# Two-layer graph attention: where three pieces of work at the crossing from layer 0 to layer 1 are issued

## The chip, the cores and the metric

The kernel runs on one core of one Trainium2 chip. The metric is the device time of one execution in microseconds, the median of several runs. A core has five engines that work side by side: TensorE (PE, matrix products into PSUM), VectorE (DVE), ScalarE (ACT), GpSimd (POOL) and SyncE (SP), whose queue here issues most transfers. Each engine executes its own instructions in the order in which the program emits them, and waits on semaphores for the others.

## What is computed

Eight batches of 2048 nodes with 256 features pass through two graph layers that share one adjacency matrix. Each is wrapped as `x = x + layer(relu(layernorm(x)))`. Layer 0 is attention with four heads, normalised separately in each chunk of 256 keys; layer 1 is attention of the additive kind, whose logit is a leaky ReLU of one number per query and one per key.

```python
h = jnp.maximum(_layernorm(x, axis=-1), 0.0)
# layer 0: q, k, v = h @ W.T; scores clipped to +-10, absent edges at -10
attn = jax.nn.softmax(scores, axis=-1)            # within each chunk of 256 keys
out = ctx @ Wo.T + bo + h
x = x + layernorm(out) * gamma + beta
# layer 1
h = jnp.maximum(_layernorm(x, axis=-1), 0.0)
hW = h @ W
e = leaky_relu(e_src[:, :, None] + e_dst[:, None, :], 0.01)
e = jnp.where(adj == 0, -1e9, e)
x = x + relu(softmax(e) @ hW)
```

A node without any edge gets equal weights in layer 1, so its output is the plain mean of `hW` over all nodes. The kernel treats these nodes apart: it adds up `h` over the nodes of a batch, multiplies the sum by `W` once, and adds the result where a node is alone.

## The kernel before

**Tiling.** Everything is done in fp32 on 128 partitions. The 2048 nodes of a batch are four blocks of 512 (called `zero`, `low`, `mid`, `last` in the main loop), a block is four tiles of 128 tokens. PSUM has eight banks in use: four in two double tiles with the tag `s` (`ps_s`; `ps_h` takes the first half of one), two with the tag `n`, two with the tag `t`. The function `ps_m` hands out `t`, or, while `turn_about` is set, `n` and `t` in turn.

**Layer 0.** `Attention.begin` (L597) and `Attention.end` (L629) emit one step of attention together: 32 steps, each 512 queries against a chunk of 256 keys. A step's products are the logits (L490), the values (L506) and the sums of exponentials (L518), all on quarter tiles of the array, so that several run at once. VectorE clips (L530), ScalarE takes exponentials (L539), GpSimd adds halves (L545), `invert` takes the reciprocal on ScalarE (L550, L551), and `scale` (L560) on VectorE multiplies values by it, which frees the `n` banks. `gather` (L565) then adds the product to the context by a transfer issued from GpSimd. `fence` (L462) puts a wait by way of SP between two groups of matmuls that write the same bank.

The steps are software-pipelined: at the end `begin(33)`, `end(33)` and `begin(34)` have no new logits and only finish values and sums of the last two steps.

**Pieces beside attention.** A dictionary `todo` holds pieces of other work by half step: `at(STEPS2 + 2, ...)` is emitted in `begin(33)`, `STEPS2 + 3` in `end(33)`, `STEPS2 + 4` in `begin(34)` and run in `end(34)`, `STEPS2 + 5` in `end(34)`. A piece marked `pe` is emitted between the exponentials and the scaling in `begin`, and in `end` ahead of the fenced second half of the sums. If there is a next batch (`ahead`), its first projections are put there as `pe` pieces, in banks from `ps_h`.

**Between the layers.** Class `Between` carries a block from its context to layer 1. `output` and `take` multiply by `Wo` and add the residual; `stats`, `power`, `shift`, `scaled`, `gamma`, `beta`, `add` are the layer norm and the addition; `stats1`, `power1`, `shift1`, `norm1` the next norm. Its result is turned to have features on partitions: either on TensorE (`turn1`, L375, and `keep1`, L786, which also adds up the features), or by `flip1`, `send1`, `fetch1`, a path through DRAM, after which `sum1` (L803 to L809) adds up each half on ScalarE. `values(t)` (L811 to L817) is the product of one token tile with the layer-1 weights, in 258 columns: the features and both attention numbers. `keep(t)` (L819) copies the features to `g` on ScalarE (L822) and the two numbers to `sd` on VectorE (L823). `ends(1)` is `values` and `keep` for all four tiles. `sum1` writes its copy over its own input, except for a block whose `flip1` was given the tag "both".

**Layer 1.** `Layer1.weights` (L936) builds four key tiles of weights at a time on VectorE in a tile of five buffers, from the source of the block (`source`, L919, on ScalarE) and the targets. `products` (L956, L963) multiplies them with `g`. There are 16 such pieces per batch, four per block; `weights(i + 2)` is emitted before `products` of piece `i`. `total` (L896) reduces the sums of features on VectorE, `mean` (L885) multiplies them by the weights on TensorE (L890) and copies the result on ScalarE (L894), and `alone` (L968) adds it on VectorE, at the third piece of each block. `early(i)` is `products` of piece `i` issued ahead of the main loop.

**Order.** The order at the crossing is written out by hand, in two branches: `if ahead` (batches one to seven) and `else` (the eighth). After the last product of a crossing, layer 1 runs in a loop over the 16 pieces, with the first steps of the next batch's attention at its end. All four compute engines and SP follow this order (`manual_schedule`).

Of the kernel before, what the change touches and what calls it, by code (L numbers as in the profile page):

```python
# [28 lines left out]
def gnn_two_layers(  # L29
# [26 lines left out]
    TB = NB // P  # L56
# [14 lines left out]
    def ps_n():  # L71
        return ps.tile([P, 512], F32, tag="n", name="ps_n")

    def ps_t():
        return ps.tile([P, 512], F32, tag="t", name="ps_t")
# [4 lines left out]
    def ps_m():  # L80
        if turn_about[0]:
            turn_about[1] += 1
            if turn_about[1] % 2:
                return ps_n()
        return ps_t()
# [128 lines left out]
    def pe(piece):  # L214

        piece.kind = "pe"
        return piece
# [161 lines left out]
    class Projection:  # L379
# [40 lines left out]
        def fetch(self, nb):  # L420
            self.hT[nb] = Features(turned_d[0][nb])
# [18 lines left out]
        def values(self, nb):  # L440
            if self.v is None:
                self.v = work.tile([P, NT, F], F32, tag="v", name="v", bufs=1)
            for t2 in range(TB // 2):
                pp = ps_m()
                for i in range(2):
                    t = 2 * t2 + i
                    for di in range(FC):
                        nc.tensor.matmul(  # L448
                            pp[:, i * F:(i + 1) * F], self.hT[nb].tokens(di, t), wvT[:, di, :],
                            start=di == 0, stop=di == FC - 1,  # L450
                        )
                t0 = nb * TB + 2 * t2
                nc.vector.tensor_tensor(
                    self.v[:, t0:t0 + 2, :], pp.rearrange("p (i f) -> p i f", i=2),
                    bv_r[:, None, :].to_broadcast([P, 2, F]), op=ALU.add,
                )
# [216 lines left out]
    class Between:  # L673
# [134 lines left out]
                    spare = self.turning.squares.rearrange("p f t b -> p (f t b)")[:, c * NB:(c + 1) * NB]  # L808
                nc.scalar.activation(spare, h, AF.Copy, accum_out=self.sums[:, self.nb, c:c + 1])  # L809

        def values(self, t):  # L811
            pp = self.pp[t] = ps_m()
            for di in range(FC):
                nc.tensor.matmul(  # L814
                    pp[:, 0:F + 2], self.hT.tokens(di, t), w1s[:, di, :],
                    start=di == 0, stop=di == FC - 1,
                )  # L817
# [182 lines left out]
    STEPS2 = 2 * STEPS  # L1000
# [46 lines left out]
    for nb in range(NNB - 1):  # L1047
        i = 6 * nb
# [69 lines left out]
    for b in range(B):  # L1118
# [3 lines left out]
        zero, low, mid, last = blocks  # L1122
        ahead = projs.get(b + 1)
        one = Layer1(b, blocks, sd, sums)
# [4 lines left out]
        def at(n, *pieces):  # L1129
            todo.setdefault(n, []).extend(pieces)  # L1130
# [46 lines left out]
        if ahead:  # L1177
            at(STEPS2 - 4, lambda: ahead.fetch(0))
            at(STEPS2 + 2, pe(lambda: ahead.tiles()), pe(lambda: ahead.qk(0, 0, ps_h)))
            at(STEPS2 + 3, pe(lambda: ahead.qk(0, 1, ps_h)), lambda: ahead.fetch(1))  # L1180
        else:
            at(STEPS2 - 4, zero.fetch1)
            at(STEPS2 + 4, zero.sum1)
        at(STEPS2 + 5, low.sum1)
        turn_about[0] = False
        for n in sorted(todo):
            if n < 4:
# [15 lines left out]
        if ahead:  # L1203
            for t in range(TB):
                mid.stats1([t])
                low.values(t)
                low.keep(t)
            zero.fetch1()
            mid.power1()
            mid.shift1()  # L1210
            mid.norm1(0)
            mid.norm1(1)
            ahead.values(0)
            ahead.fetch(2)
            last.output(0)
            last.output(1)
            mid.flip1(0, "both")
            last.take(0)
            mid.flip1(1)
            last.take(1)  # L1220
            mid.send1()
            zero.sum1()
            last.stats(range(TB))
            ahead.qk(1, 0)
            last.power()
            last.shift()
            last.scaled(range(TB))
            ahead.qk(1, 1)
            for t2 in range(2):
                last.gamma(t2)  # L1230
                last.add(t2)
            for t in range(TB):
                last.stats1([t])
                zero.values(t)
                zero.keep(t)
            mid.fetch1()
            last.power1()
            last.shift1()
            last.norm1(0)
            last.norm1(1)  # L1240
            ahead.values(1)
            ahead.qk(2, 0)
            last.flip1(0, "both")
            last.flip1(1)
            last.send1()
            ahead.fetch(3)
            mid.sum1()
            ahead.qk(2, 1)
            mid.ends(1)
            last.fetch1()  # L1250
            one.send(1)
            one.send(2)
            ahead.values(2)
            one.receive(1)
            one.targets(0, 3 * TB)
            one.sources(0)
            ahead.qk(3, 0)
            weights(0)
            ahead.qk(3, 1)
            last.sum1()  # L1260
            last.ends(1)
            one.total()
            one.targets(3 * TB, NT)
            weights(1)
            one.mean()
            one.send(3)
            ahead.values(3)
        else:
            for t in range(TB):
                zero.values(t)  # L1270
                zero.keep(t)
                mid.stats1([t])
            one.targets(0, TB)
            one.sources(0)
            mid.power1()
            mid.shift1()
            low.ends(1)
            weights(0)
            mid.norm1(0)
            mid.norm1(1)  # L1280
            one.targets(TB, 2 * TB)
            last.output(0)
            last.output(1)
            weights(1)
            last.take(0)
            last.take(1)
            mid.ends(0)
            mid.ends(1)
            last.stats(range(TB))
            last.power()  # L1290
            last.shift()
            last.scaled(range(TB))
            one.targets(2 * TB, 3 * TB)
            one.send(1)
            one.receive(1)
            accs[0] = one.accumulators(0)
            early(0)
            for t2 in range(2):
                last.gamma(t2)
                last.add(t2)  # L1300
            last.stats1(range(TB))
            last.power1()
            last.shift1()
            weights(2)
            last.norm1(0)
            last.norm1(1)
            early(1)
            last.ends(0)
            last.ends(1)
            early(2)  # L1310
            one.total()
            one.targets(3 * TB, NT)
            weights(3)
            one.mean()
            one.received(1)
            one.send(2)
            one.send(3)
            one.receive(2)
            weights(4)
# [4 lines left out]
        for i, (nb, j4) in enumerate(pieces1):  # L1324
            if not ahead and i < 3:
                continue
            if i + 2 < len(pieces1):
                weights(i + 2)
            if nb not in accs:
                accs[nb] = one.accumulators(nb)  # L1330
            if j4 == 1 and nb + 1 < NNB:
                one.received(nb + 1)
                if nb + 2 < NNB:
                    one.receive(nb + 2)
            if j4 == 2:
                one.alone(nb)
            one.products(accs[nb], ws.pop(i), j4)
            if j4 == 0 and nb > 0:
                one.finish(nb - 1, accs[nb - 1])
            if j4 == 0 and nb > 0 and nb + 1 < NNB:  # L1340
                fetch(bounds1, nb + 1)
            if ahead and (nb, j4) == (NNB - 1, 0):
                fetch(bounds, 0)
            if j4 == 1 and nb > 0:
                one.store(nb - 1)
            if far and i in (3, 6, 9, 12):
                far.send(i // 3 - 1)
            if far and i in (0, 3, 6, 9):
                far.load(i // 3)
            if far and i in (1, 4, 7, 10):  # L1350
                far.stats(i // 3, range(TB))
                far.power(i // 3)
                far.shift(i // 3)
            if far and i in (2, 5, 8, 11):
                for t2 in range(2):
                    far.norm(i // 3, t2)
                for t2 in range(2):
                    far.flip(i // 3, t2)
            if ahead and i == len(pieces1) - 4:
                att = Attention(ahead)  # L1360
            if ahead and i >= len(pieces1) - 4 and i < len(pieces1) - 1:
                att.early(i - (len(pieces1) - 4))
                if i == len(pieces1) - 2:
                    att.early(3)
# [34 lines left out]
```

## Time and profile before

| | |
|---|---|
| median of 3 runs | 3558.47 us (3555.39 to 3564.36) |
| the profiled execution's own time | 3563.89 us |
| its span in the trace | 3562.1 us |
| mean granted TensorE clock | 0.998 |
| logits L490, busy | 1431.8 us, 16384 records of 590 ns |
| values L506, busy | 1224.9 us, 16384 records of 591 ns |
| layer-1 products L963 in the s banks | 447.8 us, 2048 records of 380 ns |
| layer-1 values L814 in the t banks | 69.3 us, 256 records |
| product of the mean L890 | 8.7 us, 32 records |

Times are microseconds from the start of the span unless marked otherwise. A line of a timeline gives the start, the length, engine, source line, operation, output and inputs, shapes, and how many records were merged; in brackets stands how long the engine sat idle before it, and what ended that. One fp32 product appears as two records, and records overlap, since matmuls are pipelined: what a group costs is read from the start of one group to the start of the next. In a list of waits, "5.8, 7, 0.8" is the total, the number of times and the longest.

### The profile page before, as it was taken

To read this page: it belongs to the slowest core of one execution; us is meant where nothing else is said; L and a number is where in the kernel's file an instruction comes from. 1 tells how busy PE (TensorE), PEld (TensorE's weight loads), DVE (VectorE), ACT (ScalarE), POOL (GpSimd) and SP (SyncE) were. 2 spreads that over 40 slices of the span, in tenths; PEclk is the share of its full clock that TensorE was granted. 3 is DMA by queue.
4 is the path that set the end of the run, shared out by engine and by line. 5 is a ranking of instruction groups with operands and counts; after the bars stand their busy time and mean duration, and the time that the engine had idled before them with its cause. 6 is when DMAs were issued, how large, how long until landed. Compare 5 with 4: busy or idle time off the path is not lost.

```text
span 3562.1 us, 104433 instructions
## 1 busy us (share of the span) xinstructions
PE 3527.6 (99%) x46080; PEld 2183.0 (61%) x46080; DVE 2639.0 (74%) x3979; ACT 1947.4 (55%) x2961; POOL 1808.9 (51%) x1182
## 2 busy tenths in 40 slices
PE   8999999999999999999999999999999999999999
PEld 5455785557755577555775557655586555855568
DVE  7888677867678676786767867678586785757866
ACT  6677426763267633676236762367624766147750
POOL 2688016870278702786037850378404784048731
PEclk9999999999999999999999999999999999999999
DMA  7545423444234441344423444234442434124321
GB/s 234 119 107 134 87 74 85 91 113 91 80 79 85 123 95 60 85 96 109 92 66 85 97 110 91 71 79 91 120 103 55 91 81 118 57 55 91 85 69 48
DMA packets 169111, 329.74 MB, mean 93 GB/s; under 512 B 35664, under 2 KB 97360, under 8 KB 160464
## 3 DMA queue, kind: packets, MB, share of 16 engines
q1 hardware_dynamic: 127696, 203.51, 19.2%
q0 software_dynamic: 32640, 118.50, 18.0%
q8 instruction: 360, 5.90, 0.7%
q10 hardware_dynamic: 8320, 1.05, 0.2%
q14 instruction: 95, 0.78, 0.1%
HBM read 154.14 MB, written 51.43 MB: 58 GB/s over the span
## 4 chain that ended last, share of the span: by engine, by line
PE 97%; DVE 1%; DMA 1%; ACT 1%; issue 0%; POOL 0%; ACTq 0%; DVEq 0%; POOLq 0%; SPq 0%
PE ps_s L490 25%; PE ps_n L506 24%; PE ps_s L963 12%; PE ps_t L518 7%; PE ps_n L963 6%; PE ps_t L963 6%; PE ps_t L714 2%; PE ps_t L434 2%; PE ps_n L434 2%; PE ps_s L434 2%; PE ps_t L814 2%; PE ps_n L814 2%; PE ps_t L448 1%; PE ps_n L448 1%; DVE z L277 0%
## 5 line engine op out<-in xcount | busy, mean ns | idle before, releaser
L530 DVE SCALAR_TENSOR_TENSOR e<-ps_s,bound 128x1024 f32<-128x1024 f32 x1024 | 1224.1, 1220 | 404.0 <-PE ps_s L490 400.6
L545 POOL TENSOR_TENSOR both<-e 128x1024 f32<-128x1024 f32 x512 | 1219.8, 2407 | 571.1 <-PE ps_t L518 355.6
L490 PE MATMUL ps_s<-q,k 64*32 64x512 f32 x16384 | 1431.8, 590 | 1.5 <-DVE e L530 1.4
L539 ACT ACTIVATE e<-e 128x1024 f32<-128x1024 f32 x1024 | 1050.6, 1050 | 481.1 <-DVE e L530 462.7
L506 PE MATMUL ps_n<-e,v 64*32 64x512 f32 x16384 | 1224.9, 591 | 2.4 <-DVE prod L560 2.4
L506 PEld LDWEIGHTS ps_n<-e,v 64*32 64x32 f32 x16384 | 460.9, 107 | 473.1 <-issue 384.1
L490 PEld LDWEIGHTS ps_s<-q,k 64*32 64x32 f32 x16384 | 459.5, 106 | 448.6 <-issue 331.2
L518 PE MATMUL ps_t<-both,ones 64*32 64x512 f32 x4096 | 537.9, 592 | 0.1
L963 PE MATMUL ps_s<-g,w 128*128 128x257 f32 x2048 | 447.8, 380 | 0.0
L963 PEld LDWEIGHTS ps_s<-g,w 128*128 128x128 f32 x2048 | 388.8, 190 | 56.3
L560 DVE TENSOR_TENSOR prod<-ps_n,rz 128x512 f32<-128x512 f32 x448 | 288.5, 686 | 162.8 <-PE ps_n L506 96.1
L986 POOL TENSOR_TENSOR x<-x,r 128x256 f32<-128x256 f32 x124 | 90.7, 745 | 466.2 <-ACT r L984 465.4
L946 DVE SCALAR_TENSOR_TENSOR w<-bound,w 128x1024 f32<-128x1024 int8 x256 | 314.7, 1229 | 8.7
L354 POOL TENSOR_TENSOR krn<-krn,mv 128x4 f32<-128x4 f32 x28 | 6.8, 242 | 575.4 <-DVE w L940 575.4
L963 PE MATMUL ps_n<-g,w 128*128 128x257 f32 x1024 | 292.4, 382 | 0.0
L963 PE MATMUL ps_t<-g,w 128*128 128x257 f32 x1024 | 289.7, 380 | 0.0
L550 ACT ACTIVATE rz<-ps_t 128x512 f32<-128x512 f32 x256 | 152.6, 596 | 229.4 <-PE ps_t L518 201.5
L940 DVE TENSOR_SCALAR w<-src,cd 128x512 f32<-128x512 f32 x512 | 263.1, 556 | 7.0 <-ACT src L921 6.6
L963 PEld LDWEIGHTS ps_n<-g,w 128*128 128x128 f32 x1024 | 192.8, 190 | 44.3 <-issue 17.6
L565 POOL DMA_DIRECT2D ctxT<-prod x224 | 191.0, 853 | 54.1 <-DVE prod L560 46.7
L963 PEld LDWEIGHTS ps_t<-g,w 128*128 128x128 f32 x1024 | 193.8, 189 | 28.2
L551 ACT ACTIVATE rz<-rz 128x512 f32<-128x512 f32 x256 | 161.4, 630 | 8.2
(133 smaller groups left out, 2910.4 us busy)
## 6 DMA issues: line engine op xcount, KB each, us to landing
ctxT<-prod POOLq DMA_DIRECT2D x224, 512.0 KB, 4.9
bound<-bound_d SPq DMA_DIRECT2D x62, 1024.0 KB, 6.2
turned_d<-squares SPq DMA_DIRECT2D x232, 128.0 KB, 2.4
hT<-turned_d SPq DMA_DIRECT2D x58, 512.0 KB, 4.3
rows<-in_adj_dram SPq DMA_DIRECT2D x32, 512.0 KB, 5.3
x<-in_x_dram SPq DMA_DIRECT2D x32, 512.0 KB, 4.9
out_dram<-x SPq DMA_DIRECT2D x31, 512.0 KB, 2.6
xp<-in_x_dram SPq DMA_DIRECT2D x28, 512.0 KB, 4.5
```

The lines of the kernel that those rows point to most:

```text
L434: nc.tensor.matmul(in_key_order(pp) if i == 0 else pp, w[:, di, do * P:(do + 1) * P], h, start=di == 0, stop=di == FC - 1,)
L490: nc.tensor.matmul(self.s[n, o][c * Q:(c + 1) * Q, kt, :], self.k[p][rows, at:at + Q], self.q[p][rows, nb * NB:(nb + 1) * NB], start=True, ...
L506: made.append(nc.tensor.matmul(self.num[n, c][h * Q:(h + 1) * Q, :], self.v[rows, j * KT + kt, at:at + Q], self.e[n, p][rows, i * KT + kt, :],
L518: nc.tensor.matmul(self.total[n][h * Q:(h + 1) * Q, :], ones[rows, :], self.both[n, h // 2][rows, h % 2, :], start=half == 1, stop=half == 0,)
L530: nc.vector.scalar_tensor_tensor(self.e[n, p][:, i * KT:(i + 1) * KT, :], self.s.pop((n, o)), -CLIP * SC, bounds[nb][:, j * KT:(j + 1) * K ...
L539: nc.scalar.activation(e, e, AF.Exp, scale=1.0 / SC)
L545: nc.gpsimd.tensor_tensor(self.both[n, p], e[:, 0], e[:, 1], op=ALU.add)
L560: nc.vector.tensor_tensor(dst[:, c, :], self.num.pop((n, c)), self.rz[n], op=ALU.mult)
L565: nc.gpsimd.dma_start(self.ctxT[nb], self.prod.pop(n), accum_op=ALU.add)
L940: nc.vector.tensor_scalar(w[:, i, :], self.src[nb], self.cd[:, 0, j:j + 1], self.cd[:, 1, j:j + 1], op0=ALU.mult, op1=ALU.max,)
L946: nc.vector.scalar_tensor_tensor(two, bounds1[nb][:, j - 1:j + 1, :], 0.0, two, op0=ALU.is_gt, op1=ALU.mult)
L963: nc.tensor.matmul(accs[t][:, 0:F + 1], w[:, i, t * P:(t + 1) * P], g[:, j, :], start=j == 0, stop=j == NT - 1,)
```

## The change

Three things are issued elsewhere; nothing that is computed changes.

1. In the last batch, the layer-1 values of the first block (`zero.values` and `zero.keep` for its four tiles) become `pe` pieces of the last two attention steps, two in `begin(33)` and two in `end(33)`, with banks from `ps_h`. They leave their place after attention. `mid.stats1`, which was interleaved with them, now follows `targets` and `sources`.
2. `low.sum1` is no longer emitted at half step `STEPS2 + 5` for any batch. With a next batch it follows low's values and their copies, ahead of `zero.fetch1`. In the last batch it follows `low.ends(1)`, ahead of the first `weights(0)`; there also the two `last.take` (the residual sums) go ahead of the second weights, `weights(1)`.
3. With a next batch, `one.mean()` is emitted in layer 1 after the products of the first piece, not before `one.send(3)` and the next batch's `values(3)`. In the last batch it stays where it was.

```diff
-        def values(self, t):
-            pp = self.pp[t] = ps_m()
+        def values(self, t, bank=ps_m):
+            pp = self.pp[t] = bank()
...
         else:
+            def zero_values(t):
+                zero.values(t, ps_h)
+                zero.keep(t)
+
             at(STEPS2 - 4, zero.fetch1)
+            at(STEPS2 + 2, pe(lambda: zero_values(0)), pe(lambda: zero_values(1)))
+            at(STEPS2 + 3, pe(lambda: zero_values(2)), pe(lambda: zero_values(3)))
             at(STEPS2 + 4, zero.sum1)
-        at(STEPS2 + 5, low.sum1)
...
                 low.values(t)
                 low.keep(t)
+            low.sum1()
             zero.fetch1()
...
             weights(1)
-            one.mean()
             one.send(3)
             ahead.values(3)
         else:
-            for t in range(TB):
-                zero.values(t)
-                zero.keep(t)
-                mid.stats1([t])
             one.targets(0, TB)
             one.sources(0)
+            mid.stats1(range(TB))
             mid.power1()
             mid.shift1()
             low.ends(1)
+            low.sum1()
             weights(0)
             mid.norm1(0)
             mid.norm1(1)
             one.targets(TB, 2 * TB)
             last.output(0)
             last.output(1)
-            weights(1)
             last.take(0)
             last.take(1)
+            weights(1)
...
             one.products(accs[nb], ws.pop(i), j4)
+            if ahead and i == 0:
+                one.mean()
```

## The prediction

> **What bounds the kernel now.** I read the page's table of busy time first, then the chain of waits, then every wait of TensorE, and then the timeline of TensorE at one crossing from attention to layer 1 (the seventh batch) and at the last batch's.
>
> ```profile
> PE 3527.6 (99%) x46080; PEld 2183.0 (61%) x46080; DVE 2639.0 (74%) x3979; ACT 1947.4 (55%) x2961; POOL 1808.9 (51%) x1182
> ...
> PE 97%; DVE 1%; DMA 1%; ACT 1%; issue 0%; POOL 0%; ACTq 0%; DVEq 0%; POOLq 0%; SPq 0%
> ```
>
> TensorE is busy nearly all the time and 97% of the chain. A moved matmul costs the same elsewhere, so only time in which TensorE stands still, or runs at a lower clock, can be won. The reader is to see how few waits there are:
>
> ```profile
> PE ps_n L890 <- DVE hsum L898: 5.8, 7, 0.8
> ...
> PE ps_n L814 <- DVE o L728: 3.1, 1, 3.1
> PE ps_t L814 <- ACT hT L809: 2.4, 7, 0.3
> PE ps_n L506 <- DVE prod L560: 2.4, 2, 1.4
> ```
>
> Two waits occur 7 times, once in each batch that has a next one: the mean's product waits for the reduced sums, and the second block's values (low, L814) wait for low's sum on ScalarE. The other two lie in the last batch. A crossing with a next batch:
>
> ```profile
> 2981.45 2.27 PE L506 MATMUL ps_n<-e,v 64*32 64x512 f32 x28
> 2984.07 1.31 PE L814 MATMUL ps_t<-w1s,hT 128*128 128x258 f32 x4 [0.35 <-ACT hT L809]
> 2985.22 1.03 PE L814 MATMUL ps_n<-w1s,hT 128*128 128x258 f32 x4
> ...
> 3032.28 1.03 PE L814 MATMUL ps_t<-w1s,hT 128*128 128x258 f32 x4
> 3034.14 1.10 PE L890 MATMUL ps_n<-w1s,hsum 128*128 128x256 f32 x4 [0.83 <-DVE hsum L898]
> 3035.08 1.89 PE L448 MATMUL ps_t<-wvT,hT 128*128 128x256 f32 x8
> ```
>
> The starts matter more than the bracketed waits. The last batch's tail, and the clock granted in it:
>
> ```profile
> 3405.40 2.20 PE L506 MATMUL ps_n<-e,v 64*32 64x512 f32 x28
> 3409.04 3.68 PE L506 MATMUL ps_n<-e,v 64*32 64x512 f32 x32 [1.44 <-DVE prod L560]
> ...
> 3437.00 1.57 PE L814 MATMUL ps_n<-w1s,hT 128*128 128x258 f32 x4 [3.14 <-DVE o L728]
> ```
> ```profile
> 3406.80:3410.20 3.40, 1.96 (x32) 1.00 0.98 296
> 3410.20:3413.60 3.40, 3.40 (x32) 0.51 1.00 286
> 3413.60:3417.00 3.40, 3.30 (x28) 0.50 0.33 61
> 3417.00:3420.40 3.40, 3.40 (x32) 0.99 0.03 5
> 3434.10:3437.50 3.40, 0.50 (x2) 1.00 0.00 0
> 3437.50:3440.90 3.40, 3.40 (x9) 0.51 0.13 53
> ```
>
> (Columns of the second: stretch, length, TensorE busy, clock, DMA share, GB/s.) After each gap TensorE ran at half clock for 3.4 or 6.8 us.
>
> **What the Trainium skill says.** (1) "TensorE: Matmul & The Clock Gate", Part 1: the array's clock is either half or full, set from activity in a free-running window of 3413 ns. The trace agrees in the two values and in the length: 0.50 for two windows from 3410.2 and one from 3437.5. It differs in that a window with 1.96 us of work in it already led to the lower clock. (2) "PSUM — Partial Sum Buffer", PSUM bank collisions: the compiler back end adds a dependency between ScalarE and VectorE accesses of one bank, reads included. The trace agrees: VectorE's copy of two columns (L823) starts at 3420.59, just after ScalarE's copy of that bank (3420.20 + 0.36). (3) "Perfetto Trace Analysis", Identifying the Most-Contended Engine: matmul busy time is a poor measure because matmuls are pipelined. So I count from starts.
>
> **The mean inside layer 1 (7 batches).** From the last block's fourth L814 unit (3032.28) to the next batch's values (3035.08) are 2.80 us. A unit of L814 (one token tile, four records) lasts 0.87 from start to start (2985.22 to 2986.09), so without the mean the values could start at 3033.15: 1.93 earlier. Between products the mean takes 0.87: the last batch has it there already (starts 3466.46 and 3467.33). Net 1.06 a batch; 2.80 also stands at 410.87 − 408.07 and 846.78 − 843.98. 7 × 1.06 = 7.4 us. Cover: ScalarE's copy of the mean now waits for products(0), near 3036.6 + 6.94 = 3043.5 plus 0.87, and behind it on ScalarE waits the source of the next block, 0.71 us, done near 3045.5. VectorE needs that source for the fifth weights at 3048.1, and `alone` needs the mean at 3052.5. VectorE is also more than 10 us ahead of TensorE there (fifth weights done 3052.5, wanted near 3065). PSUM: the values take the banks of L814 copies done by 3032.5. If all cover failed, the old 1.06 would come back.
>
> **Low's sum after low's values (7 batches).** The first L814 unit takes 2984.07 to 2985.22. Unblocked it starts when the last attention values leave room: L434 followed the same x28 group after 2970.95 − 2968.81 = 2.14, stretched by 0.07 here, so at 2983.66, and a full-array unit after tiled ones costs 0.87 + 0.20 (the eight L434 after that group take 3.63 from start to start in the chain of waits, where four within a row take 1.72, eight 3.43). It ends at 2984.73: 0.49 earlier, 3.4 us in seven. What may come late instead: output's context. Its gather is issued at 2985.43 and lands 4.8 later, at 2990.2; output starts at 2991.29, in the changed kernel 2990.8. Enough, though with 0.6 us left. On ScalarE the two sums (1.22) now stand between the copies and `power1`: copies end near 2987.9, sums at 2989.2, `power1` at 2989.2 instead of 2988.90. VectorE's shift, first values, flips and takes queue behind it, 0.3 late; the bank that needs `take` first is wanted at 2997.7 and free at 2993.9. On SP, the fetch for zero reuses low's buffer: issued near 2989.3 instead of 2988.08.
>
> **The last batch.** Zero's four L814 units (3.5 us) move ahead. Two go after the values at 3405.40, into the gap before 3409.04. But their copies are queued ahead of the `scale` products on VectorE, and ScalarE's copy comes first: units at 3407.2 and 3408.07 end 3408.2 and 3409.1, the second ScalarE copy 3409.5, VectorE's 3409.7, first product done 3410.4 (0.69). TensorE's next values wait for that bank: 3410.4 instead of 3409.04. So 1.74 of work goes in, and a gap of 1.5 stays. Warm, those values take 1.7 plus 0.5 for the second bank (3412.6), sums 0.4, then the other two units (1.74) stand where TensorE now waits 0.95 for the fence (3413.58 to 3414.53), and the last sums and values take 2.15: attention ends near 3416.8, not 3418.5, with zero's values done. Then the sources, and low's four values wait for the last products' bank (3417.7) and end at 3421.3. Output wants two things: a bank, freed by a copy that ScalarE queues behind `power1` (mid's stats wait for GpSimd's add, 3420.8; copy near 3423.2 to 3424), and the context (gather near 3418.6, landing 3423.5). TensorE idles some 2.3 to 2.8. Output ends near 3427.5, mid's turn waits for ScalarE's norm (3427.8). VectorE builds weights(0) from 3424.5 to 3429.0, takes follow at once, and the 3.14 wait goes: early(0) starts near 3432.8, not 3440.09. Next late is the last block's norm on VectorE and ScalarE (stats to norm 12.4 in both): 3447.3, against TensorE free at 3446.7. Its turn starts 7.0 earlier than 3454.41. If the clock still falls after the first gap it costs up to 3.4; after the second 0.7 of 1.7, since that norm covers the rest. Bounds 2.5 to 7; I take 5.
>
> **Sum.** 7.4 + 3.4 + 5 = 15.8. The profiled execution took 3563.89 (span 3562.1, 1.8 around it): 3548.1. It stood 5.4 over the median shown, with one late feature transfer (1.3) and one late product among its waits; from the median 3558.47, 3543.
>
> **Rivals.**
> (a) All three pay, 12.5 to 20 us: 3538.5 to 3546, centre 3543. Chance 0.62.
> (b) Low's wait is only replaced, by output's context (0.6 us of room, and gathers landed after 4.7 to 5.0), or the tail stays at half clock: 7.4 + 3 to 7.4 + 5, 3546 to 3550. For it: the room; against it: output never waited. 0.24.
> (c) The tail gains nothing, because zero's copies hold back the last products, and low's wait comes back: 7.4 alone, 3551. 0.08.
> (d) Slower. Zero's features land late. Their fetch now waits for low's sum to free the buffer, and zero's sum stands on ScalarE ahead of the next projection's evictions (2996.66). It decides once a landing exceeds 6 us (2989.3 + 6 + 1.2 = 2996.5). Near 12, as one feature transfer took (11.9 at 2144), evictions and the last block's power come some 5 late; TensorE has four banks of 1.72 each, less part of it, so it loses about 4. In seven batches 28 − 15.8 = 12: 3570. Against it: this fetch took 3.7. 0.06.
>
> **How the numbers follow.** Runs of before spread from 3555.39 to 3564.36, so 0.3% (10.7 us) is about what can be told from no change. Faster by more means below 3547.8: all of (a), half of (b), 0.74. Within: the rest of (b) and (c), 0.20. Slower: 0.06. The range holds (a) and most of (b), with 2 us for the median's own scatter: 3536 to 3552.
>
> **What would show it.** Right: no wait of L890 on hsum; next-batch values 0.87 after the last L814 unit; no L814 wait on L809; in the tail two L814 units ahead of the gap, no wait on L728, output waiting for bank or context. Wrong: output with a DMA wait in all batches, a larger wait at L506, half clock for more windows, or fetches for zero over 6 us.

## The result, and the profile after

The changed kernel took 3544.55 us (median of 5 runs, 3543.62 to 3548.03), the kernel before 3558.47. The ratio is 0.9961, with a 95% interval of 0.9948 to 0.9975: 13.9 us less, or 0.39%. The profiled execution took 3546.50, with a span of 3544.7, which is 17.4 us below the span before.

The page's first line, and TensorE's waits (total, times, longest) in the changed kernel:

```profile
PE 3518.3 (99%) x46080; PEld 2185.4 (62%) x46080; DVE 2637.4 (74%) x3979; ACT 1946.3 (55%) x2961; POOL 1808.7 (51%) x1182
```
```profile
...
PE ps_n L506 <- DVE prod L560: 3.5, 4, 1.4
PE ps_n L692 <- DVE sd L823: 3.1, 1, 3.1
PE ps_s L490 <- DVE e L530: 1.4, 1, 1.4
PE ps_n L814 <- ACT hT L786: 0.7, 2, 0.3
...
```

Both waits that occurred seven times are gone: TensorE no longer waits for `hsum` or for the sum L809. The wait of 3.14 for `take` (L728) is gone too, and a new one of 3.05 stands at output (L692). The crossing of the seventh batch in TensorE's timeline:

```profile
2971.16 2.27 PE L506 MATMUL ps_n<-e,v 64*32 64x512 f32 x28
2973.36 1.14 PE L814 MATMUL ps_t<-w1s,hT 128*128 128x258 f32 x4
2974.34 1.10 PE L814 MATMUL ps_n<-w1s,hT 128*128 128x258 f32 x4
...
3021.47 1.03 PE L814 MATMUL ps_t<-w1s,hT 128*128 128x258 f32 x4
3022.34 1.89 PE L448 MATMUL ps_n<-wvT,hT 128*128 128x256 f32 x8
```
```profile
3025.79 7.10 PE L963 MATMUL ps_s<-g,w 128*128 128x257 f32 x32
3032.73 1.03 PE L890 MATMUL ps_n<-w1s,hsum 128*128 128x256 f32 x4
3033.59 18.61 PE L963 MATMUL ps_s<-g,w 128*128 128x257 f32 x85
```

From the attention values (x28) to the first layer-1 product the crossing now takes 3025.79 − 2971.16 = 54.63, where it took 3038.53 − 2981.45 = 57.08. Of the 2.45, the mean pays 3033.59 − 3032.73 = 0.86 back between the products: a net 1.59 a batch, 11.1 in seven. The other six crossings lie within 0.11 of 54.63; before, they lie within 0.24 of 57.08, except one of 58.66 with a late transfer in it.

The last batch's tail:

```profile
3393.25 2.20 PE L506 MATMUL ps_n<-e,v 64*32 64x512 f32 x28
3395.38 2.01 PE L814 MATMUL ps_s<-w1s,hT 128*128 128x258 f32 x8
3398.76 2.52 PE L506 MATMUL ps_n<-e,v 64*32 64x512 f32 x32 [1.37 <-DVE prod L560]
...
3414.47 1.99 PE L692 MATMUL ps_n<-woT,ctxT 128*128 128x256 f32 x8 [3.05 <-DVE sd L823]
...
3442.13 7.10 PE L963 MATMUL ps_s<-g,w 128*128 128x257 f32 x32
```

Two of zero's units (x8) stand ahead of the gap, and the gap is still there. Call the time from the x28 values to the third early product (the last line) the tail: 48.88 us here, 3459.53 − 3405.40 = 54.13 before. Behind it both traces have 102.57 us. So the two spans differ by 5.25 in the tail and 12.15 ahead of it; of these, 11.1 are the seven crossings and 1.35 a transfer that landed late before; other waits ahead of the tail differ in both directions, among them 1.53 by which the changed kernel came to its first crossing later. The clock stayed at 1.00 in the tail; before, it was at half for 10.2 us.

### The profile page after: what moved, and what is told of

It reads as the page before. It is cut to its first block, busy times and chain, and to the rows that moved or that the text cites. A ratio compares the mean times of both kernels' runs of the same rounds, so it can differ in the third digit from the quotient of the medians.

```text
span 3544.7 us, 104427 instructions
## 1 busy us (share of the span) xinstructions
PE 3518.3 (99%) x46080; PEld 2185.4 (62%) x46080; DVE 2637.4 (74%) x3979; ACT 1946.3 (55%) x2961; POOL 1808.7 (51%) x1182
## 4 chain that ended last, share of the span: by engine, by line
PE 97%; DVE 1%; DMA 1%; ACT 0%; issue 0%; POOL 0%; DVEq 0%; POOLq 0%; ACTq 0%
PE ps_s L490 25%; PE ps_n L506 25%; PE ps_s L963 13%; PE ps_t L518 7%; PE ps_n L963 6%; PE ps_t L963 6%; PE ps_t L714 2%; PE ps_t L434 2%; PE ps_n L434 2%; PE ps_s L434 2%; PE ps_t L448 2%; PE ps_n L448 2%; PE ps_t L814 2%; PE ps_n L814 2%; PE ps_n L692 0%; PE ps_t L692 0%
## 5 line engine op out<-in xcount | busy, mean ns | idle before, releaser
L354 POOL TENSOR_TENSOR krn<-krn,mv 128x4 f32<-128x4 f32 x28 | 6.8, 242 | 570.6 <-DVE w L940 570.6
```

## The experiments

Nine other kernels were run, and the kernels before and after once more. The tail was read from each trace, since single runs of one kernel differ by up to 13 us. The gains in us are worked out from the ratios as they were recorded, which are not quite the quotients of the medians: in the first run below, the medians differ by 9.0 where the ratio gives 10.3.

**The mean alone.** The kernel before with only this:

```diff
             weights(1)
-            one.mean()
             one.send(3)
...
             one.products(accs[nb], ws.pop(i), j4)
+            if ahead and i == 0:
+                one.mean()
```

> The kernel before with part 3 alone: the mean's product goes into layer 1 in the seven batches that have a next one. Theory: the wait for the reduced sums goes and 0.87 us of product comes back between products, 1.06 a batch, so 7.4 us in all, near 3551 against 3558.5. From the last L814 unit to the next batch's values 0.87 instead of 2.80. Rival, the product only moves its wait (to ScalarE's source or the products' bank): within 1 us of the kernel before.

3551.42 against 3560.41, ratio 0.9971 (0.996 to 0.9981): 10.3 us less, interval 6.8 to 14.2. Crossings without another wait take 55.15, 1.93 less than 57.08, and 0.87 comes back: 1.06 a batch, 7.4 in all, as expected and inside the interval.

**Low's sum alone.** The kernel before with

```diff
-        at(STEPS2 + 5, low.sum1)
+        if not ahead:
+            at(STEPS2 + 5, low.sum1)
...
                 low.keep(t)
+            low.sum1()
             zero.fetch1()
```

> The kernel before with low's sum behind low's values in the seven batches that have a next one; the last batch as before. Theory: 0.5 us a batch, 3.5 us in all, near 3555; no wait of L814 on L809, and output still without a wait. Rival, the wait is replaced by output's context or by a late fetch for zero: 0 to 1 us, or slower by several us.

3556.48 against 3560.41, ratio 0.9988 (0.9982 to 0.9995): 4.3 us less, interval 1.8 to 6.4. The fourth L814 unit starts 4.99 after the x28 values, not 5.52, and a crossing without a late transfer takes 56.55, not 57.08: 0.53 a batch, 3.7 in seven. Output has no wait. Two feature transfers landed late in this trace; such waits (0.9 to 3.7 us a run) are in some runs of either order and absent in others.

**The last batch alone.** The changed kernel with the mean and low's sum back in their old places where there is a next batch:

```diff
+        if ahead:
+            at(STEPS2 + 5, low.sum1)
...
                 low.keep(t)
-            low.sum1()
...
             weights(1)
+            one.mean()
...
-            if ahead and i == 0:
-                one.mean()
```

> The kernel with the last batch's part alone (zero's values inside attention, low's sum behind low's values there, take ahead of the second weights); the seven other crossings as in the kernel before. Theory: 5.2 us less, near 3553, all of it between the values at which the kernel before idles 1.44 us and the third early products. Rival, the parts need each other (an earlier crossing shifts transfers): clearly less than 5, or the three single parts do not add up to the 14 us of the whole.

3558.49 against 3560.41, ratio 0.9996 (0.9988 to 1.0004): 1.4 us less, interval −1.4 to 4.3. A miss: the whole interval lies below 5.2. The trace shows where it went. The order of the instructions in the tail is that of the changed kernel, and so is every gap, but output ran at half clock:

```profile
3426.76 3.68 PE L692 MATMUL ps_n<-woT,ctxT 128*128 128x256 f32 x8 [3.06 <-DVE sd L823]
```
```profile
3426.00:3426.50 0.50, 0.00 (x0) 1.00 0.00 0
3426.50:3427.00 0.50, 0.24 (x1) 0.90 0.00 0
3427.00:3427.50 0.50, 0.50 (x2) 0.50 0.00 0
...
3430.00:3430.50 0.50, 0.50 (x4) 0.69 0.00 0
3430.50:3431.00 0.50, 0.50 (x4) 1.00 0.00 0
```

(Second fence: stretch, length, TensorE busy, clock.) The clock falls to 0.50 for 3.4 us, one window. The same gap of 3.05 in the changed kernel's first trace was followed by 1.00. So the tail's length is partly chance, and both kernels were run once more.

**Both kernels again.**

> The kernel before, once more, for its last batch's stretch alone (from the values at L506 x28 ahead of the 1.44 us gap to the third early products). That stretch took 54.1 us in the first trace with three windows at half clock, 51.4 and 52.2 in the two experiments that leave it as it was, with fewer. Theory: where the clock's windows fall against the gaps is chance, so it lies between 49.6 (no window at half clock) and 54.5 again, and its excess over 49.6 follows the time at half clock. Rival, the stretch has one length and the 54.1 is it.

> The changed kernel, once more, for the same stretch, which took 48.9 us in its first trace with no window at half clock and 50.6 in the experiment with the last batch's part alone, with one window at half clock in output. Theory: one of these two lengths or between, by chance. Rival: always 48.9.

These two executions took 3560.41 and 3545.40 us. The tail of before fell between the bounds named; that of the changed kernel took 48.88 again, as the rival had it. All traces of the two tails, with the time at half clock in the tail (twice the clock's deficit, summed over 1 us stretches):

| tail as in | run | tail us | at half clock us |
|---|---|---|---|
| before | first trace | 54.13 | 10.2 |
| before | low's sum alone | 52.24 | 6.8 |
| before | mean alone | 51.42 | 3.4 |
| before | again | 51.05 | 3.4 |
| changed | last batch alone | 50.57 | 3.4 |
| changed | first trace | 48.88 | 0 |
| changed | again | 48.88 | 0 |

At full clock the changed tail takes 48.88 in both its traces; it was not seen with a window itself, but the kernel with the last batch alone has the same instructions there, and its one window costs 50.57 − 48.88 = 1.69. The old tail had one to three windows in each of four traces, and its gap of 3.14 was followed by one in all of them. The units after that gap show the cost; in the repeat,

```profile
3433.51 1.85 PE L814 MATMUL ps_n<-w1s,hT 128*128 128x258 f32 x4 [3.14 <-DVE o L728]
3435.16 1.93 PE L814 MATMUL ps_t<-w1s,hT 128*128 128x258 f32 x4
3436.88 14.20 PE L963 MATMUL ps_s<-g,w 128*128 128x257 f32 x64
```

the two units take 3.37 from start to start, where two units after a gap take 1.85 at full clock (in the kernel with take behind the second weights, below), and the products 14.04 instead of 13.87. Less these 1.7, the old tail would last 49.4; the same sum gives 49.7 with the mean alone and 49.4 with low's sum alone. No trace showed it without a window, so this is an estimate: at full clock the new order is worth 0.5 to 0.8 us. The rest is fewer windows at half clock. Between single traces the gain lies anywhere from 51.05 − 50.57 = 0.48 to 5.25; the means of the table differ by 52.2 − 49.4 = 2.8.

**Filler.** The kernel before with four extra products of zero's tiles in banks from `ps_h`, where the change puts zero's values; nobody reads them.

```diff
...
+            at(STEPS2 + 2, pe(lambda: filler(0)), pe(lambda: filler(1)))
+            at(STEPS2 + 3, pe(lambda: filler(2)), pe(lambda: filler(3)))
             at(STEPS2 + 4, zero.sum1)
```

> The kernel before with four extra products of zero's tiles, whose results nobody reads, at the two places where the change puts zero's values; zero's own values stay where they were. 3.5 us of TensorE work more. Theory: the gaps and the half clock that followed them were worth as much, so the stretch from those values to the sources grows by at most 0.5 us and the clock stays at 1.00; time as before. Rival, the clock plays no part and only the gaps are filled: 1.5 us or more longer, with the half clock still there.

3561.05 against 3558.42, ratio 1.001 (1.0001 to 1.0019): 3.6 us more, interval 0.4 to 6.8. In the trace the first gap is gone (the extra units are L1185), and the clock stays at 1.00 up to the sources L931:

```profile
3400.54 2.20 PE L506 MATMUL ps_n<-e,v 64*32 64x512 f32 x28
3402.68 2.01 PE L1185 MATMUL ps_s<-w1s,hT 128*128 128x258 f32 x8
3404.62 2.08 PE L506 MATMUL ps_n<-e,v 64*32 64x512 f32 x32
...
3416.30 0.49 PE L931 MATMUL ps_t<-ident,sd 128*128 128x128 f32 x3
```

This stretch takes 15.76. In the kernel before it took 16.88 in the first trace, with half clock, and 13.92 in the repeat (3404.98 to 3418.90), without. So against a full-clock run, the gaps hide 3.5 − 1.84, about half of the filler, and against the first trace more than all of it. The figure of at most 0.5 held only against the first trace; of the rival, the length is right and the half clock wrong. On the clock this run decides nothing: three of the four traces of the old order have full clock up to the sources too, with the gap in place.

**Take behind the second weights.** The changed kernel with

```diff
-            last.take(0)
-            last.take(1)
             weights(1)
+            last.take(0)
+            last.take(1)
```

> The changed kernel with last.take behind the second weights again. Theory: mid's third L814 unit waits for take, which VectorE reaches 4.3 us later; it would start near 2.5 us later, so 2.5 us are lost, 3.5 to 4 if the clock falls after that gap. Rival, the last block's norm (VectorE, ScalarE) sets the end of this stretch whatever TensorE does before it: 0 to 0.5 us.

```profile
3424.33 1.14 PE L814 MATMUL ps_n<-w1s,hT 128*128 128x258 f32 x4 [2.41 <-DVE o L728]
```

The wait for `take` is back and the tail is 51.55, 2.67 longer, without half clock: as expected. The time was 3547.84 against 3558.42, ratio 0.997 (0.996 to 0.998). So of the three edits to the tail, this one carries a visible length of its own. Without it the other two leave a tail of 51.55 at full clock, which is longer than the estimate of 49.4 for the old one. By that estimate, zero's values inside attention and low's later sum did not shorten the tail by themselves.

**Two more orders, and both.** In the first, zero's copies follow `scale`; in the second, low's values and copies go ahead of mid's statistics:

```diff
             def zero_values(t):
                 zero.values(t, ps_h)
-                zero.keep(t)
...
+            at(STEPS2 + 2, lambda: zero.keep(0), lambda: zero.keep(1))
...
+            at(STEPS2 + 3, pe(lambda: zero.keep(2)), pe(lambda: zero.keep(3)))
```
```diff
+            low.ends(1)
             mid.stats1(range(TB))
             mid.power1()
             mid.shift1()
-            low.ends(1)
             low.sum1()
```

> The changed kernel with zero's copies behind the products (scale) that free the attention banks; nothing else. Theory: VectorE no longer waits for the copies first, the attention values start 1.9 us earlier and the gap of 1.37 us goes; context, GpSimd's add and statistics follow, so 1.9 us less. Rival, the end of the stretch does not hang on the end of attention: 0 to 0.5 us less.

> The changed kernel with low's values and copies ahead of mid's statistics, power and shift in the last batch. Theory: output's wait for a bank (3.05 us) ends about 1.1 us earlier, at the context's landing, but VectorE starts the weights at the same time as before, so the last block's norm comes only 0.2 us earlier and the total is 0.2 to 0.3 less, unseen in the times. Rival, that wait is on the path: 1.1 us less from the values at L506 to the third early products.

> The changed kernel with two edits in the last batch: zero's copies go behind the products (scale) that free the attention banks, and low's values with their copies go ahead of mid's statistics, power and shift. Theory: the 1.4 us gap at L506 goes, since the first product is done about 1.9 us earlier, and everything behind it moves by that; output's 3.05 us wait for a bank goes too but buys only 0.2 to 0.3, since VectorE's chain of weights, take and the last block's statistics sets the next meeting point. 2.1 us less than the changed kernel, near 3542.5. Rival, the wait for the bank is on the path: 3 us less.

With the copies behind `scale` the gap of 1.37 is gone: from the x28 values to the sources 11.63 us instead of 13.47, so 1.84 less, as expected. The whole tail is 48.72, though, only 0.16 less, because output ran at half clock for one window in this trace. The time was 3545.86 against 3558.42, ratio 0.9967 (0.9954 to 0.998).

With low ahead, output's wait falls from 3.05 to 1.71, and yet the tail is 49.35, 0.47 longer, at full clock:

```profile
3408.24 1.97 PE L692 MATMUL ps_n<-woT,ctxT 128*128 128x256 f32 x8 [1.71 <-DVE mv L344]
...
3413.43 0.33 PE L375 MATMUL ps_n<-ident,hn 128*128 128x128 f32 x1 [0.17 <-ACT hn L366]
...
3414.53 1.28 PE L814 MATMUL ps_n<-w1s,hT 128*128 128x258 f32 x4 [0.34 <-ACT hT L786]
```

Mid's statistics now queue on VectorE behind low's last copy, so mid's norm (L366) starts 22.94 after the x28 values, not 21.62. Its turn (L375) waits for it, and mid's first unit starts 26.16 after them, just as in the changed kernel: what output won is lost again. The first weights start 21.85 after the x28 values (3410.22 − 3388.37), not 21.29 (3414.54 − 3393.25), and the last block's norm follows them; that is the 0.47. So another chain did take over, as expected, but the 0.2 to 0.3 that it was to leave did not come. That output's wait is off the path is not shown by this, since the same edit made mid's norm later. The time was 3544.80, ratio 0.9965 (0.9951 to 0.9978).

Both together give a tail of 47.63 at full clock, 1.25 less than the changed kernel's, not 2.1: 1.84 less, 0.47 more, and 0.13 more because attention's x32 values took 2.07 from start to start here and 1.94 with the copies alone. 3546.44 against 3560.41, ratio 0.9956 (0.9943 to 0.997).

**Additions ahead of the gather.** What held the copies that output waits for? In the changed kernel, VectorE's shift L354 on 128x4 elements:

```profile
3412.71 1.63 DVE L354 TENSOR_TENSOR rn<-rn,mv 128x4 f32<-128x4 f32 x1 [0.84 <-ACT rn L350]
3412.77 1.54 POOL L759 TENSOR_TENSOR x<-x,beta_r 128x512 f32<-128x512 f32 x1
3414.27 0.15 DVE L823 COPY sd<-ps_n 128x2 f32<-128x2 f32 x1
```

It ends when GpSimd's last addition ends (3412.77 + 1.54), and the copies queue behind it. The last kernel has the copies behind `scale`, and moves GpSimd's last four additions of the tail ahead of the last gather:

```diff
-                at((nb + 1) * PER + n, *pieces)
+                m = (nb + 1) * PER + n
+                at(m if ahead else min(m, STEPS2 + 3), *pieces)
...
-        at(STEPS2 + 3 + late, lambda: last.bias(1))
-        at(STEPS2 + 4, lambda: last.beta(0))
-        at(STEPS2 + 5, lambda: last.beta(1))
+        at(STEPS2 + 3, lambda: last.bias(1))
+        at(STEPS2 + 4 if ahead else STEPS2 + 3, lambda: last.beta(0))
+        at(STEPS2 + 5 if ahead else STEPS2 + 3, lambda: last.beta(1))
```

> The kernel with zero's copies behind scale, and in the last batch also GpSimd's last additions (mid's second half, last's bias and beta) ahead of the last gather, in the 5 us in which GpSimd stood idle before it. Theory: mid's statistics and shift no longer wait for them, so low's copies free output's bank by the time the context lands; output's wait shrinks from 3.05 to about 2, mid's norm and the second takes come 1 to 2.5 us earlier. From the values at L506 (x28) to the third early products 46 us against 48.9 of the changed kernel at full clock: 3 us less, near 3542. Rival, the context's landing and TensorE's own order hold output and mid's turn where they are: only the 1.8 of the copies, 47.

```profile
3408.43 0.16 DVE L354 TENSOR_TENSOR rn<-rn,mv 128x4 f32<-128x4 f32 x1 [0.84 <-ACT rn L350]
```
```profile
3410.44 1.97 PE L692 MATMUL ps_n<-woT,ctxT 128*128 128x256 f32 x8 [1.77 <-DMA ctxT<-prod]
```

The shift takes 0.16, as it also did with low ahead, where the additions had ended 0.7 before it. Output waits for the context alone, and the tail is 45.80 (3392.27 to 3438.07), as expected and 3.08 less than the changed kernel's. Output starts 18.17 after the x28 values instead of 21.22, so 3.05 earlier: 1.77 because attention ends earlier, 1.28 because its wait is shorter. All of it comes off the tail. So output's wait was on the path, with mid's norm close behind it, which this edit also brings earlier (18.31 after the x28 values instead of 21.62). 3543.48 against 3557.53, ratio 0.9956 (0.9942 to 0.997): faster than the kernel before, and not to be told from the changed kernel (0.9961) in the times.

## Why the prediction held, step by step

The time forecast was 3543 and the profiled execution 3548.1; they came out at 3544.55 and 3546.50, where the case that all three parts pay was put. The two parts in the seven crossings are shown by their own runs; the third is only in part what was foreseen.

- **The mean: 7.4 us.** Right in mechanism and size: 1.06 a batch where it was done alone. The cover named on ScalarE and VectorE held, for no TensorE wait appeared at the products behind it.
- **Low's sum: 3.4 us.** Right; 0.53 a batch where 0.49 was worked out, 3.7 in all. Output's context was in time, with no wait, although its room had shrunk.
- **The last batch: 5 us.** The profiled pair gives 5.25, but this agreement is partly luck: done alone, this part measured 1.4 by the times, with an interval that ends at 4.3. Two terms in it were off. First, the changed tail at full clock was to be 7.0 shorter than the traced tail of before, and was 5.25 shorter. Zero's first two units started 2.13 after the x28 values, not 1.8, so the gap behind them ended 0.5 later; and the attention groups without logits beside them were costed too short. The first sums took 0.99 from start to start, not 0.4, and the last sums and values 2.71, not 2.15, so attention with zero's values ended 0.36 later in the tail than before (13.47 against 13.11), not 1.7 earlier. Second, the 2 us then taken off for a half clock in the changed kernel did not occur in its trace, while the trace of before held more half clock than any other run of the same order. Over four traces of the old tail and three of the new one the gain is 2.8, and by the estimate above most of it is fewer windows at half clock, not gaps that were filled.
- **The gap at `scale`.** Foreseen: 1.5, measured 1.37, with the first products held by zero's copies. The experiment with the copies behind `scale` confirms the cause.
- **Output's new wait.** Foreseen at 2.3 to 2.8 with bank or context as its end; it is 3.05 and the bank is the end. That GpSimd's additions hold the shift was not in the prediction.
- **Take ahead of the second weights.** Foreseen as the end of the 3.14 wait; undoing it cost 2.67. The last block's norm, which was to come last behind it, was in time: its turn starts at 3437.01 without a wait.
- **The slow rival,** late features of zero behind low's sum, did not occur in the changed kernel's trace. Features of the last block did land late in some runs, but in both orders.

The parts add up to the difference of the medians, 7.4 + 3.7 + 2.8 = 13.9, but the last figure of this sum means little: the interval of that difference is 8.9 to 18.5, and the three parts measured by their times give 10.3 + 4.3 + 1.4 = 16.0.

## What to carry to other kernels

When one engine is busy 99% of the time, list its waits by count: here a wait of 0.83 us that returned in seven batches was worth 7.4 us, more than the waits of 1.4 and 3.1 at the end, and its gain can be worked out from the starts of the instructions around it. Work moved into a gap brings its copies with it; place them behind what the next work on the bottleneck is waiting for. Ending a wait pays only as far as no other chain is made later by the same edit: with low ahead, output's wait was 1.3 shorter, but mid's norm came 1.3 later and nothing was won. Moving the additions that held both shortened the tail by all that output won. And where a gap may or may not be followed by half clock, one pair of profiles can't price the gap.

## What the runs showed of the hardware

- Gaps of 1.4 to 3.1 us in TensorE's work are followed by half clock in some executions and not in others: after the old order's gap of 3.14 it came in all five traces with that gap (the filler's is the fifth), after output's gap of 3.05 in two of five, after the gap of 1.35 to 1.71 ahead of the attention values in one of nine (the trace of before, 1.44). The Trainium skill ("TensorE: Matmul & The Clock Gate", Part 1) describes a free-running window, so that the phase is chance; that fits, but its statement that the clock falls after an idle window is stricter than the trace of before, where 1.96 us of 3.40 were busy. There the clock also stayed low for a second window, although TensorE was busy for all 3.40 us of the first. Which windows fall was not settled.
- A VectorE operation on 128x4 elements took 0.16 us with GpSimd idle and 1.63 beside GpSimd additions, ending with the last (1.16 in the trace of before, where the addition at 3424.56 + 1.53 ended with it too). The Trainium skill ("GPSIMD Engine Reference", Key points) says that GpSimd shares its SBUF interfaces with VectorE, with contention for operations that have two SBUF inputs; the runs agree, and show that the small operation can last until the large one's end.
